# Graph network in four layers: search work kept out of layer 0's drain, row loads issued singly in it, and the scale table computed before the feature gathers

## The chip, the cores and the metric

The kernel runs on one core of a Trainium2 chip. The core has five engines that work side by side, each with its own queue of instructions, which it takes in order: TensorE (PE, matrix products), VectorE (DVE), ScalarE (ACT), GpSimd (POOL) and SyncE (SP, which here only issues transfers). Transfers between memory and the chip run on 16 DMA engines, which all queues share. The metric is the device time of one execution in microseconds, as a median over runs.

## The reference

There are 2708 nodes with 128 features each, and a sparse adjacency matrix with values between 0.05 and 1. Four graph layers follow one another, each of the form x = layernorm(x + layer(x)):

```
layer 0:  hw = x @ W0;  e = leaky_relu((pos @ hw) @ a1)     # pos = adj > 0; nothing is negative
          x = LN(x + (softmax over neighbours of e, times adj) @ hw)
layer 1:  A = adj + I;  D = rowsum(A)
          x = LN(x + relu(D^-1/2 A D^-1/2 (x @ W1.T + b1)))
layer 2:  four-head attention, logits + (1 - adj) * (-1e9)
          x = LN(x + attention(x))
layer 3:  gelu(s_i + d_j + b) for every edge, weighted by adj, summed; an update; two layer norms
```

Layers 0 and 1 are computed with the dense matrix. Layer 2 and layer 3 need each node's neighbours as a list: a row's largest entries and where they stand. Finding these lists is the kernel's "search", and the row sums D for layer 1 come out of it too.

## The kernel before

**Blocks and passes.** Nodes are cut into 22 blocks of 128 rows (`NB`), the output columns into six chunks of 512. A dense layer is done in two passes over the matrix, each accumulating some chunks in PSUM: chunks 0-2 and 3-5 in layer 0, chunks 0-3 and 4-5 in layer 1 (`PASSES`). `half_of(layer, h, ...)` is one pass: for n in 0..21 it multiplies row block n (tile `ah`) with the block's weights; `each(n, ...)` adds what else belongs to a step; `end` does a little work after the first chunk. The second pass holds back the last four row blocks (the first pass, one) and takes them chunk by chunk, so that chunks are complete one after another.

**Row loads.** `load_ahead(limit)` issues loads of row blocks into seven buffers (`BUFFERS`), as far as `limit`. Layer 0's rows and those of layer 1's second pass go through SP's queue. Those of layer 1's first pass are rows in the order of degree, so they are gathered by POOL with an indirect DMA (L728, 1.05 MB each). POOL is in order: a load whose buffer isn't free holds up all that is behind it.

**Finishing.** `finish(layer, blocks, sT)` is a generator that takes four blocks of a complete chunk through the rest of the layer, piece by piece: transposes back on PE (L635), the addition to X on DVE with the row sums (L649, "last sums" in the change), mean on POOL, squares on ACT (L257), the root on POOL (L262), the norm on ACT (L267), transposes on PE (L664), and the projection for the next layer. In layer 0 this projection is written to DRAM as `TH` through ACT's queue (L707); in layer 1 `TA` is written by ACT and `TS`, row by row in order of degree, by POOL (L693). The finishes of a first pass (`later`) run during the steps of the second pass, each starting some steps after the one before. The finishes of the second pass (`drain`) run after it; this stretch is called the drain here. `step()` moves each of them by two pieces.

**Search.** `entries(...)` is one long generator. For each block of rows in order of degree, POOL gathers the full rows (`nat`, L536, 1.39 MB, four buffers), DVE finds the eight largest entries (MAX8, L558; for blocks up to 9 in pieces, L565), the row's sum SD (L577), and the positions of the entries (FIND_INDEX8, L580; two such searches for blocks 1 to 9, three for block 0, one from block 10). After a block's first index search the load of the row block three further on is issued. `search(n)` spends a credit of n; one credit is about one of these 3 us operations. Which search work stands where on DVE's queue is thus fixed by the credits given at each place.

**Layer 1's first pass.** Its weights are the features `HS`, gathered by POOL from TH in order of degree (`features`, L861) and multiplied on ACT by DS = D^-1/2 (`weights`, L866). `given(blocks)` makes DS for some blocks, from SD by a multiply on DVE (L856) and a power on POOL (L857), and calls `search` until their sums are there. In step n the pass gathers features n + 4, gives some search credit, makes DS for blocks n + 2 and n + 3 on even n, and scales features n + 1.

**What fixes the order.** Most instructions go through `pinned(...)`, which ties each to the one before it on its engine, so their order is that in which the program emits them. The stores TH, TA and TS and SP's loads are not pinned; the framework places these as their inputs become ready. Waits come from data and buffers alone.

Of the kernel before, what the change touches and what calls it, by code (L numbers as in the profile page):

```python
# [69 lines left out]
def sparse_path(  # L70
# [29 lines left out]
    NB = -(-N // P)  # L100
# [8 lines left out]
    BUFFERS = 7  # L109
# [490 lines left out]
    with (  # L600
# [23 lines left out]
        def scaled(jb):  # L624

            pinned(S_.activation(H[:, jb, :], H[:, jb, :], AF.Copy, scale=f[:, jb : jb + 1]))  # L626

        def finish(layer, bs, sT):


            n = len(bs)
            g = slice(bs[0], bs[-1] + 1)
            o = pt.tile([P, BANK], F32, name="o_ps")
            for j in range(n):
                pinned(T_.transpose(o[:, blk(j)], sT[:, blk(j)], ident))  # L635
            yield
            if layer:
                y = sb.tile([P, 4, D], F32, name="y1")
                for j, b in enumerate(bs):

                    pinned(V_.scalar_tensor_tensor(
                        y[:, j, :], H2[:, b, :], 1.0, o[:, blk(j)], ALU.mult, ALU.add
                    ))
                for j, b in enumerate(bs):
                    pinned(S_.activation(
                        y[:, j, :], y[:, j, :], AF.Relu, scale=dinv[:, b : b + 1]
                    ))
            for j, b in enumerate(bs):
                pinned(V_.scalar_tensor_tensor(  # L649
                    X[:, b, :], y[:, j, :] if layer else o[:, blk(j)],  # L650
                    1.0 if layer else RZ[:, b : b + 1], X[:, b, :], ALU.mult, ALU.add,
                    accum_out=SUM[:, b : b + 1],
                ))
            squares, norm = norm_sums(bs)
            yield
            yield
            squares()
            yield
            yield
            norm()  # L660
            yield
            o = pt.tile([P, BANK], F32, name="o_ps")
            for j, b in enumerate(bs):
                pinned(T_.transpose(o[:, blk(j)], X[:, b, :], ident))  # L664
            yield
            xt = small.tile([P, BANK], F32, name="xt")
            pinned(S_.copy(xt[:, : n * P], o[:, : n * P]))
            yield
            if layer:

                K = D + 2 * HEADS
                ts = []
                for k in range(0, n, 2):
                    m = min(2, n - k)
                    t = pt.tile([P, BANK], F32, name="q_ps")[:, : 2 * K]
                    ts.append((k, m, t.rearrange("p (b k) -> p b k", k=K)))
                    for i in range(m):
                        pinned(T_.matmul(
                            ts[-1][2][:, i, :], xt[:, blk(k + i)], W2, start=True, stop=True
                        ))  # L680
                yield
                for k, m, t in ts:
                    b = bs[0] + k
                    pinned(S_.copy(XP[:, b : b + m, :], t[:, :m, :]))
                yield
                yield
                nc.scalar.dma_start(
                    TA[bs[0] * P : (bs[-1] + 1) * P, :].rearrange("(b p) c -> p b c", p=P),
                    XP[:, g, : D + HEADS],
                )  # L690

                for b in bs:
                    i = G_.indirect_dma_start(  # L693
                        TS, bass.IndirectOffsetOnAxis(ap=RANK[:, b : b + 1], axis=0),
                        XD[:, b, :], None,
                    )
                    tc.declare_no_dep(i.ins, group="TS", reason="each row has a place of its own")
                    tc.add_to_no_dep_group("TS", i.ins)
            else:

                t = pt.tile([P, BANK], F32, name="q_ps").rearrange("p (b k) -> p b k", k=D)
                for i in range(n):
                    pinned(T_.matmul(t[:, i, :], ONES, B1, start=True, stop=False))
                    pinned(T_.matmul(t[:, i, :], xt[:, blk(i)], W1, start=False, stop=True))
                yield
                pinned(S_.copy(H2[:, g, :], t[:, :n, :]))
                nc.scalar.dma_start(  # L707
                    TH[bs[0] * P : (bs[-1] + 1) * P, :].rearrange("(b p) d -> p b d", p=P),
                    H2[:, g, :],
                )  # L710
            yield
# [3 lines left out]
        loaded, done = [], [0]  # L715
# [24 lines left out]
        def half_of(layer, h, weights, each, end, later):  # L740


            half = PASSES[layer][h]
            lo, hi = span_of(layer, h)
            acc = [
                (pa if i < 3 else pz).tile([P, BANK], F32, name="acc" if i < 3 else "z")
                for i in range(len(half))
            ]
            base = (2 * layer + h) * NB

            def product(n, a, i):
                w = min(BANK, hi - lo - i * BANK)
                pinned(T_.matmul(  # L753
                    acc[i][:, :w], weights[:, n, :], a[:, i * BANK : i * BANK + w],
                    start=n == 0, stop=n == NB - 1,
                ))

            steps = [((1 + 3 * i if layer else 1 + 4 * i), finish(*args)) for i, args in enumerate(later)]
            last = []
            for n in range(NB):  # L760
                now = [s for k, s in steps if k <= n]
                a = loaded[base + n]
                if n < NB - (4 if h else 1):
                    for i in range(len(half)):
                        product(n, a, i)
                else:
                    last.append((n, a))
                each(n, a, lo, hi)
                if not last:
                    done[0] = base + n + 1  # L770
                    load_ahead(base + n + BUFFERS - 1)
                for s in now:
                    next(s, None)
            ends, drain = [], [s for _, s in steps]

            def step():
                for s in list(drain):
                    if next(s, 0) == 0 or next(s, 0) == 0:
                        drain.remove(s)

            for i, c in enumerate(half):
                for m, (n, a) in enumerate(last):
                    product(n, a, i)
                    if not layer:
                        search(0.28)
                    if layer or m % 2:
                        for g in drain:
                            next(g, None)
                w = min(N, (c + 1) * BANK) - c * BANK
                sT = short if w < BANK else sb.tile([P, BANK], F32, name="sT", bufs=4)  # L790
                pinned(S_.copy(sT[:, :w], acc[i][:, :w]))
                ends.append((layer, range(c * 4, min(NB, c * 4 + 4)), sT))
                if i == 0:
                    end()
                if h:
                    drain.append(finish(*ends[-1]))
            done[0] = base + NB
            load_ahead(base + NB + BUFFERS - 1)
            while drain:
                step()  # L800
                if not layer:
                    search(0.55)
            return [] if h else ends

        RZ = lists.tile([P, NB], F32, name="RZ")
        later = []
# [3 lines left out]
        for h, half in enumerate(PASSES[0]):  # L810
# [13 lines left out]
            def each0(n, a, lo, hi, h=h, behind=behind, pattern=pattern):  # L824
                if h == 0 and n + 2 < NB:
                    scaled(n + 2)
                m = signs[n % 2]
                if h and n < 2:
                    nc.gpsimd.memset(m[:, hi - lo :], 0.0)
                pinned(S_.activation(m[:, : hi - lo], a, AF.Sign))  # L830
                if behind:
                    pattern()
                behind.append((n, m))
                if h == 0 and n == 0:
                    order(pt, nat)
                    next(passes)
                if h or n >= 8:
                    search(0.85 if h else 0.8)

            def end0(z=z, blocks=blocks, pattern=pattern):  # L840
# [9 lines left out]
            later = half_of(0, h, H, each0, end0, later)  # L850
# [15 lines left out]
            pinned(S_.activation(HS[:, k, :], HS[:, k, :], AF.Copy, scale=DS[:, k : k + 1]))  # L866

        EARLY = 4
        for k in range(4):
            features(k)  # L870
        given(range(EARLY))
        weights(0)
        for h in range(2):

            def each1(n, a, lo, hi, h=h):
                if h:
                    return
                if n + 4 < NB:
                    features(n + 4)
                search(0.96)  # L880
                k = n + 2
                if EARLY <= k < NB and k % 2 == 0:
                    given(range(k, k + 2))
# [203 lines left out]
    with (  # L1087
# [173 lines left out]
        for k in range(NB):  # L1261
# [8 lines left out]
            if k:  # L1270
                added(k - 1)
                i, j = place[k]
# [526 lines left out]
```

## Time and profile before

| | us |
|---|---|
| median of three runs | 708.85 |
| lowest and highest | 706.58, 709.79 |
| the profiled execution | 709.3 |
| its span, first to last instruction | 707.5 |
| busy in it: PE, DVE, ACT, POOL | 451.2, 393.0, 272.4, 378.5 |

In the profile's time, layer 0's second pass ends with its last products at about 173 us; layer 1's first product starts at 221.75; its first pass ends at about 301; and the gathers of layer 2 begin on POOL at 362.90. A profile lists, for each engine, instructions with their start, length, line in the kernel, output and inputs; the idle time in front of one is put down to the engine or DMA that released it last. The chain of waits follows the execution back from its last instruction, each time to what released the one before.

### The profile page before, as it was taken

What the parts mean: (1) busy time and instruction counts of PE and PEld (TensorE: products, weight loads), DVE (VectorE), ACT (ScalarE), POOL (GpSimd) and SP (SyncE); (2) the same over time, 40 slices, a digit from 0 to 9 for tenths busy, and PEclk for the clock granted to TensorE, in tenths of its full rate; (3) what the DMA queues carried; (4) which work ended last, traced back from release to release, by engine and by line L of the source; (5) the groups of instructions that cost most, each with busy time, mean ns of one, the idle gap of its engine ahead of it and who ended that gap; (6) DMA issues with size and microseconds to landing.
All of it is one profiled execution on the core that took longest, in us unless ns stands there. A gap on an engine that the chain in (4) does not pass through costs nothing.

```text
span 707.5 us, 8193 instructions
## 1 busy us (share of the span) xinstructions
PE 451.2 (64%) x2565; PEld 301.7 (43%) x2565; DVE 393.0 (56%) x1138; ACT 272.4 (38%) x719; POOL 378.5 (53%) x449
## 2 busy tenths in 40 slices
PE   5889999996164999997511502066646546747461
PEld 5745445663152444464311501055536435545451
DVE  4767999999983856640208834111171251434466
ACT  3145655772330100174411574055335424444330
POOL 7002001221246776036577677777777777777761
PEclk9579999998556999999755555566776857788665
DMA  9968999996294999875254111222122122211210
GB/s 296 406 245 309 415 415 379 324 374 224 101 386 153 419 418 415 311 216 191 85 181 128 42 52 40 53 54 52 52 53 55 53 53 53 53 52 52 54 48 13
DMA packets 44400, 128.68 MB, mean 182 GB/s; under 512 B 7983, under 2 KB 19523, under 8 KB 38716
## 3 DMA queue, kind: packets, MB, share of 16 engines
q0 software_dynamic: 16832, 75.13, 30.2%
q1 hardware_dynamic: 21116, 49.66, 19.7%
q10 hardware_dynamic: 6400, 3.29, 1.7%
q8 instruction: 22, 0.36, 0.2%
q14 instruction: 30, 0.25, 0.1%
HBM read 119.29 MB, written 8.81 MB: 181 GB/s over the span
## 4 chain that ended last, share of the span: by engine, by line
DVE 27%; POOL 24%; PE 19%; issue 14%; DMA 9%; ACT 6%; SPq 0%; POOLq 0%; DVEq 0%; ACTq 0%
POOL G L1150 17%; PE acc L753 12%; DVE IX L580 9%; DVE cand L565 5%; DMA G<-TD,LIDX 4%; PE z L753 3%; POOL ga L918 2%; DMA TOP<-in_high 1%; POOL TS L693 1%; ACT squares L257 1%; PE w_ps L355 1%; ACT XD L267 1%; ACT X L1061 1%; DMA nat<-in_adjo,PERM 1%; POOL ln_r L262 1%
## 5 line engine op out<-in xcount | busy, mean ns | idle before, releaser
L1150 POOL DMA_INDIRECT G<-TD,LIDX x187 | 177.4, 948 | 58.7 <-issue 52.4
L1143 PE MATMUL aT_ps<-W,M 128*128 128x128 f32 x418 | 91.0, 394 | 112.5 <-ACT M L1180 105.1
L1143 PEld LDWEIGHTS aT_ps<-W,M 128*128 128x128 f32 x418 | 80.9, 292 | 126.4 <-ACT M L1180 114.0
L1179 DVE TENSOR_TENSOR M<-G,sd_ps 128x1152 f32<-128x1152 f32 (+11 forms) x22 | 28.3, 1287 | 159.0 <-DMA G<-TD,LIDX 142.8
L753 PE MATMUL acc<-ah,XD 128*128 128x512 f32 (+1 forms) x264 | 113.7, 568 | 1.0 <-ACT XD L626 1.0
L580 DVE FIND_INDEX8 IX<-V,nat 128x8 uint32<-128x2707 f32 x33 | 97.8, 2970 | 0.0
L830 ACT ACTIVATE sign<-ah 128x1536 bf16<-128x1536 f32 (+1 forms) x44 | 57.7, 1327 | 37.1 <-issue 26.8
L753 PE MATMUL acc<-ah,HS 128*128 128x512 f32 x132 | 63.3, 615 | 12.1 <-ACT HS L866 12.1
L753 PEld LDWEIGHTS acc<-ah,XD 128*128 128x128 f32 x264 | 47.9, 196 | 44.5 <-issue 41.4
L536 POOL DMA_INDIRECT nat<-in_adjo,PERM x22 | 21.5, 979 | 81.5 <-DVE IX L580 55.4
L1171 ACT ACTIVATE W<-TAB,V 128x128 f32<-128x128 f32 x187 | 56.8, 390 | 0.0
L558 DVE MAX8 V<-nat 128x8 f32<-128x2707 f32 x12 | 35.7, 2976 | 26.6 <-DMA nat<-in_adjo,PERM 26.6
L1180 ACT ACTIVATE M<-sd_ps 128x128 f32<-128x128 f32 x22 | 6.1, 278 | 113.2 <-DVE M L1179 113.2
L753 PEld LDWEIGHTS acc<-ah,HS 128*128 128x128 f32 x132 | 25.4, 196 | 44.7 <-issue 29.3
L866 ACT ACTIVATE HS<-HS,DS 128x128 f32<-128x128 f32 x22 | 8.4, 399 | 78.0 <-DMA HS<-TH,PERM 48.8
L565 DVE MAX8 cand<-nat 128x8 f32<-128x338 f32 (+3 forms) x88 | 34.3, 461 | 2.8 <-DMA nat<-in_adjo,PERM 2.8
L251 POOL TENSOR_SCALAR ln_a<-SUM 128x4 f32<-128x4 f32 (+1 forms) x12 | 2.9, 238 | 61.1 <-DVE XD L649 33.2
L1250 POOL DMA_INDIRECT out_x<-yo,PERM x22 | 22.1, 1003 | 18.5 <-DVE yo L1229 11.3
L861 POOL DMA_INDIRECT HS<-TH,PERM x22 | 21.0, 957 | 19.6 <-DMA TH<-H 10.1
L1052 POOL DMA_INDIRECT TD<-yd,PERM x22 | 24.2, 1102 | 9.6 <-ACT yd L1048 4.1
L753 PE MATMUL acc<-ah,H 128*128 128x512 f32 (+1 forms) x88 | 28.1, 462 | 0.0
L693 POOL DMA_INDIRECT TS<-XD,RANK x22 | 21.6, 982 | 11.3 <-issue 5.4
(281 smaller groups left out, 862.6 us busy)
## 6 DMA issues: line engine op xcount, KB each, us to landing
ah<-in_adjL SPq DMA_DIRECT2D x22, 768.0 KB, 13.5
ah<-in_adjR SPq DMA_DIRECT2D x44, 330.0 KB, 5.5
TOP<-in_high SPq DMA_DIRECT2D x5, 1354.0 KB, 13.0
ah<-in_adjL SPq DMA_DIRECT2D x22, 256.0 KB, 7.2
G<-TD,LIDX POOLq DMA_INDIRECT x187, 2.5
OWN<-TS SPq DMA_DIRECT2D x3, 798.0 KB, 8.5
TA<-XD ACTq DMA_DIRECT2D x5, 264.0 KB, 2.8
TH<-H ACTq DMA_DIRECT2D x5, 256.0 KB, 10.2
```

The costliest lines, as they stand in the source:

```text
L558: pinned(nc.vector.max(V[:, b, 0:8], t))
L565: pinned(nc.vector.max(c[:, 8 * k : 8 * k + 8], t[:, at]))
L580: pinned(nc.vector.max_index(IX[:, b, s], V[:, b, s], t))
L693: i = G_.indirect_dma_start(TS, bass.IndirectOffsetOnAxis(ap=RANK[:, b : b + 1], axis=0), XD[:, b, :], None,)
L753: pinned(T_.matmul(acc[i][:, :w], weights[:, n, :], a[:, i * BANK : i * BANK + w], start=n == 0, stop=n == NB - 1,))
L830: pinned(S_.activation(m[:, : hi - lo], a, AF.Sign))
L1052: i = G_.indirect_dma_start(TD, bass.IndirectOffsetOnAxis(ap=PERM[:, b : b + 1], axis=0), yd[:, i, :], None)
L1143: pinned(T_.matmul(t, a, b, start=n == 0, stop=n == len(parts) - 1))
L1150: pinned(G_.indirect_dma_start(G[:, s, :], None, TD, bass.IndirectOffsetOnAxis(ap=LIDX[:, b, s : s + 1], axis=0),))
L1171: pinned(S_.activation(W[:, s, :], ident, AF.Copy, scale=V[:, b, s : s + 1]))
L1179: pinned(V_.tensor_tensor(M[:, :n, :], G[:, :n, :], s_, ALU.add))
L1250: i = G_.indirect_dma_start(out, bass.IndirectOffsetOnAxis(ap=PERM[:, b : b + 1], axis=0), h, None, bounds_check=N - 1, oob_is_err=False,)
```

## The change

In layer 0's second pass search credit is given only up to step 17, none while the last products are taken chunk by chunk; in the drain it is given from the point where all three finishes have added their sums, one credit per step instead of 0.55. The loads of layer 1's first row blocks are no longer issued together ahead of the drain, but at most one after each of its steps, with the rest after it. The first four blocks' DS is made before the first four feature gathers are issued. In the steps of layer 1's first pass the credit is 1.1 instead of 0.96. The finishes that run during layer 1's second pass start four steps apart instead of three.

```diff
+        added_up = [0]
+
         def finish(layer, bs, sT):
...
                     accum_out=SUM[:, b : b + 1],
                 ))
+            added_up[0] += 1
             squares, norm = norm_sums(bs)
...
-            steps = [((1 + 3 * i if layer else 1 + 4 * i), finish(*args)) for i, args in enumerate(later)]
+            steps = [(1 + 4 * i, finish(*args)) for i, args in enumerate(later)]
...
+            added_up[0] = 0
             for i, c in enumerate(half):
                 for m, (n, a) in enumerate(last):
                     product(n, a, i)
-                    if not layer:
+                    if not layer and not h:
                         search(0.28)
...
             done[0] = base + NB
-            load_ahead(base + NB + BUFFERS - 1)
+            if not h:
+                load_ahead(base + NB + BUFFERS - 1)
             while drain:
                 step()
-                if not layer:
-                    search(0.55)
+                load_ahead(min(base + NB + BUFFERS - 1, len(loaded) + 1))
+                if not layer and added_up[0] >= len(half):
+                    search(1.0)
+            if h:
+                load_ahead(base + NB + BUFFERS - 1)
             return [] if h else ends
...
-                if h or n >= 8:
+                if n < 18 if h else n >= 8:
                     search(0.85 if h else 0.8)
...
         EARLY = 4
+        given(range(EARLY))
         for k in range(4):
             features(k)
-        given(range(EARLY))
         weights(0)
...
-                search(0.96)
+                search(1.1)
```

## The prediction

> **What bounds the kernel now.** I read the page first, then busy time by stages, the chain of waits, and each engine's instructions in order of time from 150 to 366 us. The page gives the time to move, and by the DMA row (40 slices of 17.7 us, in tenths) where transfers are full: slices 3-8 and 13-15, with a hole in 10 and 12 between:
>
> ```profile
> span 707.5 us, 8193 instructions
> DMA  9968999996294999875254111222122122211210
> ```
>
> By stages (columns: stretch, its length, then busy us and instruction count of PE, PEld, DVE, ACT, POOL, then granted clock, DMA share, GB/s):
>
> ```profile
> 175.00:180.00 5.00, 0.00 (x0) 0.00 (x0) 4.76 (x15) 0.00 (x0) 0.00 (x0) 0.53 0.51 214
> 205.00:210.00 5.00, 4.56 (x20) 4.02 (x19) 4.93 (x5) 1.21 (x4) 0.38 (x1) 0.55 1.01 392
> 210.00:215.00 5.00, 0.00 (x0) 0.00 (x0) 2.40 (x3) 0.07 (x1) 0.00 (x0) 0.79 0.68 254
> 215.00:220.00 5.00, 0.00 (x0) 0.00 (x0) 4.45 (x6) 0.00 (x0) 3.62 (x4) 0.50 0.14 39
> 240.00:250.00 10.00, 10.00 (x25) 4.40 (x24) 8.34 (x7) 1.10 (x3) 8.06 (x10) 1.00 1.02 419
> 280.00:285.00 5.00, 5.00 (x13) 2.28 (x12) 2.84 (x1) 0.00 (x0) 2.07 (x3) 1.00 1.00 407
> ```
>
> Two stages, two limits. From 173 to 221 PE has almost nothing: the first product of layer 1 waits for layer 0's drain. From 225 to 295 PE is full and so are the DMA engines, at about 418 GB/s. The drain in the chain of waits (start, us, what):
>
> ```profile
> 179.99 2.76 issue
> 182.75 1.15 DVE XD L649 x8
> ...
> 210.10 4.51 DMA TH<-H
> ...
> 220.21 1.06 POOL DS L857
> ```
>
> And the end of layer 1's first pass, in the instructions in order of time (start, us, instruction, then idle time before it and its releaser):
>
> ```profile
> 282.16 2.98 DVE L558 MAX8 V<-nat 128x8 f32<-128x2707 f32 x1 [2.94 <-DMA nat<-in_adjo,PERM]
> ...
> 289.26 0.71 POOL L857 TENSOR_TENSOR DS<-SD,HALF 128x2 f32<-128x2 f32 x1 [5.90 <-DVE SD L856]
> ...
> 292.74 0.40 ACT L866 ACTIVATE HS<-HS,DS 128x128 f32<-128x128 f32 x1 [3.20 <-DMA HS<-TH,PERM]
> ```
>
> PE had the transposes for blocks 12-15 ready at 169.8, but DVE, 13 us behind with search, added them at 182.75. The last feature store (TH) left at 210.10. Later, block 21's row came at 282.16, its scale at 289.97; PE's step 20 waited for gathered features until 293.1. So that scale has only 2.8 us to spare.
>
> **What the skill says.** DMA: Bandwidth & Descriptors, "Queues, rings and completion order": each DMA engine takes turns between queues, packet by packet, so small stores share with big loads. The trace agrees: the TH store issued at 203.25 landed after 10.2 us, beside row loads that ended at 213.1; the last, at 210.10, landed with them gone at 214.61. Same page, "Where 436 GB/s comes from": a ceiling of 435; the trace's 419 is near it, so bytes moved into 225-295 cost time. TensorE: Matmul & The Clock Gate, "Part 1: The HAM clock gate": an idle window of some 3.4 us halves the clock and as much work restores it. Trace: 0.50 at 215-225, 1.00 from 230.
>
> **The change, part by part.**
>
> *Search out of the drain.* Between block 8's candidates and the last sums, before ran on DVE: two index searches each of blocks 8 and 9 and one of block 10 (5 x 2.97), candidates of 9 (4.2), MAX8 of 10 (2.97), about 22 us. After, DVE is free at 165.5. Walking the queues with the trace's durations: add 12-15 at 170.0-171.1, sums on POOL to 171.7, ACT squares (behind a copy of sums that ends at 172.1) to 173.6, POOL roots 1.6 to 175.3, norms 1.65 to 177.0, squares 16-19 to 178.5, roots to 180.2, norms to 181.9; PE transposes and products as before (1.6 + 3.4 a group at half clock, 1.7 for the last pair). Last TH issue about 191 instead of 210.1: 19 us.
>
> *Row loads one by one.* Before, five loads stood on POOL at 192.5-198.6 ahead of the roots of 16-19. After, load 1 follows the last sums at 181.1, then nat 11, and the last pair's root; loads 2-4, nat 12 (after block 9's first index search, 189.1) and load 5 end at about 191.5. But 5 x 1.05 + 2 x 1.386 = 8.0 MB then fill the DMA from 182.6: 19.2 us at 418 GB/s, to about 202.5. All three TH stores fall into that. They crawl as at 203.25 and land at about 204.3, not 196. Gain at the first feature gather 215.47 - 205.2 = 10.3 us, not 19. Lower bound of that landing: 197 (191 plus the 6.5 us of the store at 207.76); upper: 207.
>
> *Scale table first.* Its POOL power (1.06) now waits for DVE through block 10's MAX8, 195; the gathers are queued behind it, but wait for TH until 204 anyway, so it costs nothing. It takes 1.3 us of POOL from behind the gathers, so gather 4 moves from 221.45 to about 210.3: 11.1 us gained. Were TH to land at once, this wait would set a floor of 196.
>
> *What moved into layer 1.* At its start before had MAX8 of block 12 behind it, after only that of block 10: four DVE operations (12 us) and nat loads 13 and 14 move in. Credit 1.1 instead of 0.96: 1.1 x 3.1 = 3.4 us of DVE a step, against PE's 3.43: DVE isn't the limit in between. But nat 21 is issued in step 15, not 13. Ahead of it in POOL's queue are 2 more nat, 2 more row and 2 more feature loads: 2 x (1.386 + 1.049 + 0.066) = 5.0 MB = 12.0 us. SP's loads for the next pass start when step 15's product frees a buffer, and now overlap it: about 3 of 0.34 MB, 2 us. Nat 21 lands at 282.16 - 11.1 + 12.0 + 2.0 = 285.1. From there as before 7.8 us (MAX8, index, scale, power): 292.9, step 20 at 293.4 against 293.29. The lead is eaten. And since PE finished step 19 some 8 us earlier, its clock falls: step 20 takes 5.3 instead of 3.43, +1.9. End of the pass: +2.0 us.
>
> *Layer 1's finishing every 4 steps.* PE's queue is in order. Before, the transposes of 12-15 stood before step 17 and ran at 333.0 behind POOL's stores TS (5.1 us a group); the four last products of chunk 4 ended at 339.8. After, that finish starts at step 13, not 10: its root, norm, transposes and projection stand just before those four products. Laying out POOL, ACT and PE by the same durations (step 1.105, norms 1.65, relu 1.28, root 1.64, stores 1.26 each) gives, for before, sums of 16-19 at 344.2 (trace 344.6). For after, on the same origin: norms of 12-15 at 335.1, chunk 4's copy at 343.0 instead of 339.6, sums of 16-19 at 346.2: +2.0. PE idles less in mid-pass, but step 17 was not the end. The stores aren't pinned; I place them as the trace does, as soon as their projection is copied. If they interrupt less, the cost is -0.5; if they stand behind the sums, +6.4. I take +2.0.
>
> The remaining edits are free: in layer 1's second pass no rows are left to load, so the load calls between its drain's steps issue nothing, and SP's queue keeps its order everywhere.
>
> The terms no trace shows, with both ends: TH's landing 197 to 207 (nat 21 7 us earlier to 3 later; but a pass more than some 6 us shorter is barred by the features, which then bind), SP's overlap 0 to 3, the clock 0 to 1.9, finishing -0.5 to +6.4. All at one end: 709.3 - 6 - 0.5 = 703, and 709.3 + 2.0 + 2.7 + 1.0 + 6.4 = 721.
>
> Sum: 709.3 for the profiled execution (span 707.5 and 1.8 around it) + 2.0 + 2.0 = 713.3; the median 708.85 is 0.45 below that execution, so 712.9.
>
> **Rivals.** (1) *The lead survives; not slower.* If TH stores slip between the loads and land near 198, everything to nat 21 comes 6 us earlier, step 20 is then bound by its feature gather, PE idles less and keeps its clock: pass -4 to -6, finishing 0 to +2. Time 705, down to 701. For it: at 208 us most of a group's store went through within 1 us, with a load pending. Against: from 157 to 161 stores and loads in one queue after another moved side by side, 10.2 and 15.0 us to land. It decides where TH lands before 201. (2) *The layer 1 spacing costs more*: stores behind the sums, +6.4 instead of 2: 717, and 719 with TH at 207. For it: four operations of a finish queue behind POOL's 5.1 us blocks. Against: before's stores went out early. (3) *It cancels*: stores and clock cost nothing, 709. (4) *DVE is no hindrance*: the drain was bound elsewhere, no gain: then before's 13 us lag would not show; 3 in 100, about 717.
>
> **Numbers.** Forecast 712.9 has 0.42 (its own range 710 to 716), rival 1 0.25, rival 2 0.17, rival 3 0.13, rival 4 0.03. A measurement tells about 0.5%, 3.5 us, from no change: faster 0.25; same, rival 3 and two fifths of the forecast, 0.30; slower 0.45. Range 701 to 719 leaves out some 0.15.
>
> **What would show it.** Right: adds of 12-15 near 170; last TH issue near 191 but landing beyond 202; first gather near 205; nat 21 landing near 285 and DVE the last wait of step 20, clock below 1 after it; TS stores ahead of sums. Wrong: TH landing below 199, step 20 waiting for its features, or chunk 4's copy no later after the pass's start.

## The result, and the profile after

The changed kernel takes 717.06 us, the median of four runs (714.57 to 717.35); the kernel before, beside it, 707.72 (706.3 to 709.79). The ratio is 1.0117, 95% interval 1.0097 to 1.0137: slower by 9 us. The forecast was 712.9 with a range of 701 to 719, some 4 us more than before. Its direction and its chain of causes were right; two terms of its sum were too small. The profiled execution took 717.35 with a span of 715.6, 8.1 more than the span before.

The events the forecast named, in us from the start of the span:

| event | before | forecast | after |
|---|---|---|---|
| PE's transposes of blocks 12-15 done | 169.8 | as before | 171.5 |
| DVE adds blocks 12-15 | 182.75 | 170.0 | 171.5 |
| last TH store issued | 210.1 | 191 | 190.1 |
| TH landed | 214.6 | 204.3 | 207.4 |
| first feature gather issued | 215.5 | 205.2 | 208.3 |
| search row of block 21 landed | 282.2 | 285.1 | 288.8 |
| step 20 of layer 1's first pass | 293.2 | 293.4 | 297.1 |
| second pass begins | 300.9 | 302.9 | 307.0 |
| chunk 4 copied, after that beginning | 39.1 | 42.1 | 44.6 |
| sums of blocks 16-19, after that beginning | 43.7 | 45.3 | 48.0 |

In the first row this execution is 1.7 us late. PE waits for nothing there; eight products from 162.36 took 6.64 us, before 5.15, because the granted clock in 165-170 was 0.67 instead of 0.99. It is scatter and not the change: in the twelve executions of the changed kernel and of its variants below, none of which is edited ahead of that place, DVE's first add came anywhere from 169.94 to 172.79. So differences of absolute times under some 2 to 3 us between two traces say little; those from one event to another in the same trace are firmer.

The page of the kernel after, span and transfers (40 slices of 17.9 us):

```profile
span 715.6 us, 8195 instructions
DMA  9968999990669999476227111222122222211210
```

Counted from 0, slice 9 (161 to 179 us) now moves almost nothing; 10 and 11 stand at six tenths, where before 10 stood at two, 11 at nine and 12 at four; transfers are full from 12 to 15 instead of 13 to 15. The stages show the same (columns as before: length, then PE, PEld, DVE, ACT, POOL, then clock, DMA share, GB/s):

```profile
180.00:185.00 5.00, 4.17 (x19) 4.17 (x20) 5.00 (x7) 3.67 (x12) 3.36 (x7) 0.50 0.00 0
...
200.00:205.00 5.00, 0.00 (x0) 0.00 (x0) 4.93 (x5) 0.00 (x0) 0.00 (x0) 0.50 1.02 421
205.00:210.00 5.00, 0.00 (x0) 0.00 (x0) 4.93 (x7) 0.00 (x0) 1.40 (x2) 0.50 0.34 135
210.00:215.00 5.00, 3.64 (x5) 1.58 (x6) 2.16 (x2) 1.49 (x4) 3.78 (x5) 0.50 0.20 52
...
280.00:285.00 5.00, 2.66 (x6) 1.25 (x7) 4.63 (x5) 0.40 (x1) 1.08 (x2) 1.00 1.04 423
```

PE's drain is over by 190, 20 us sooner. Then PE has nothing for 21 us, for 17 of which the transfers run at some 421 GB/s. And in 280-285, where before PE was full, it now works 2.66 us of 5, with the DMA engines still full. The chain of waits names both places:

```profile
190.06 17.37 DMA TH<-H
...
272.99 15.81 DMA nat<-in_adjo,PERM
288.82 2.99 DVE V L558
...
295.93 0.73 POOL DS L865
...
297.13 4.97 PE acc L756 x6
```

The last TH store takes 17.37 us beside the row loads; before, issued after them, it took 4.51. At the end of the pass stands block 21's row, 15.81 us on its way, and behind it DVE and POOL. The instructions behind that row in order of time (start, us, instruction, idle time and its releaser):

```profile
292.18 2.97 DVE L580 FIND_INDEX8 IX<-V,nat 128x8 uint32<-128x2707 f32 x1
295.68 0.16 DVE L864 TENSOR_SCALAR SD<-SD 128x2 f32<-128x2 f32 x1
295.93 0.72 POOL L865 TENSOR_TENSOR DS<-SD,HALF 128x2 f32<-128x2 f32 x1 [13.30 <-DVE SD L864]
297.13 2.07 PE L756 MATMUL acc<-ah,HS 128*128 128x512 f32 x2 [7.62 <-ACT HS L874]
```

PE stands for 7.62 us. Its six products of that step then take 4.97 us instead of 2.84: the clock has fallen, to 0.50 in 295-300. Earlier in the pass PE had already waited three times for gathered features that were late, 1.49 us at 263, 1.52 at 272 and 3.02 at 282; in the kernel before it waited for nothing between its first product and the second pass. The index search at 292.18 stands ahead of the scale although the scale doesn't use it.

The second pass, before and after, in the same view, cut to the instructions that matter here; TS are POOL's stores, `ln_a` the means of a finish, and the x10 the products that stand behind the finish of 12-15 and end chunk 4:

```profile
323.62 0.23 POOL L251 TENSOR_SCALAR ln_a<-SUM 128x4 f32<-128x4 f32 x1
336.39 3.85 PE L753 MATMUL acc<-ah,H 128*128 128x512 f32 x10
340.02 0.58 ACT L791 COPY sT<-acc 128x512 f32<-128x512 f32 x1 [3.05 <-DMA TA<-XD]
344.63 0.27 POOL L251 TENSOR_SCALAR ln_a<-SUM 128x4 f32<-128x4 f32 x1
```

and after:

```profile
327.53 0.96 POOL L696 DMA_INDIRECT TS<-XD,RANK  x1 [0.30 <-issue]
328.51 0.28 POOL L251 TENSOR_SCALAR ln_a<-SUM 128x4 f32<-128x4 f32 x1
336.92 0.96 POOL L696 DMA_INDIRECT TS<-XD,RANK  x1 [0.30 <-issue]
337.90 0.27 POOL L251 TENSOR_SCALAR ln_a<-SUM 128x4 f32<-128x4 f32 x1
342.44 1.63 PE L667 MATMUL o_ps<-TAB,XD 128*128 128x128 f32 x4 [4.74 <-ACT XD L267]
346.72 5.11 PE L756 MATMUL acc<-ah,H 128*128 128x512 f32 x10
351.61 0.58 ACT L795 COPY sT<-acc 128x512 f32<-128x512 f32 x1 [4.26 <-PE acc L756]
354.97 0.23 POOL L251 TENSOR_SCALAR ln_a<-SUM 128x4 f32<-128x4 f32 x1 [2.67 <-DVE XD L651]
```

The means of blocks 12-15 ran 22.7 us after the pass began (323.62); now they run 30.9 us after it (337.90), directly behind four stores, and PE waits 4.74 us for their norm with the last products of chunk 4 still to come. After that wait PE is slow as well: the projection took 2.18 us instead of 1.09 and those ten products 5.11 instead of 3.85, with a clock of 0.58 in 345-350. The last `ln_a` line of each list is the mean of 16-19, the last row of the table.

By the parts: the first pass ends 6.1 us later, the second is 4.3 longer, and 2.2 come back after layer 1: from the first table gather to the end of the span it is 344.6 us before and 342.4 after. The eight executions below on chips of this speed, with edits only ahead of that place, took 340.8 to 343.8, so the profiled execution of before was itself a slow one there.

### The profile page after: what moved, and what is told of

Read it like the earlier page. It is cut to its first block, busy times and chain, and to the rows that moved or that the text cites. A ratio compares the mean times of both kernels' runs of the same rounds, so it can differ in the third digit from the quotient of the medians.

```text
span 715.6 us, 8195 instructions
## 1 busy us (share of the span) xinstructions
PE 453.4 (63%) x2565; PEld 300.8 (42%) x2565; DVE 393.1 (55%) x1138; ACT 272.8 (38%) x719; POOL 379.1 (53%) x449
## 4 chain that ended last, share of the span: by engine, by line
POOL 25%; PE 24%; DMA 20%; issue 13%; DVE 11%; ACT 6%; SPq 1%; POOLq 0%; DVEq 0%; ACTq 0%
POOL G L1158 17%; PE acc L756 17%; DMA ah<-in_adjL,PERM 6%; DMA G<-TD,LIDX 4%; DMA TOP<-in_high 3%; DMA TH<-H 2%; POOL ga L926 2%; DMA nat<-in_adjo,PERM 2%; PE z L827 2%; ACT squares L257 2%; POOL ln_r L262 1%; ACT X L1069 1%; ACT XD L267 1%; DVE M L1187 1%; PE aT_ps L1151 1%
## 5 line engine op out<-in xcount | busy, mean ns | idle before, releaser
L756 PE MATMUL acc<-ah,HS 128*128 128x512 f32 x132 | 65.5, 634 | 35.4 <-ACT HS L874 35.4
L731 POOL DMA_INDIRECT ah<-in_adjL,PERM x22 | 21.5, 979 | 13.7 <-issue 5.0
L926 POOL DMA_INDIRECT ga<-TA,LIDX x22 | 23.9, 1085 | 6.7 <-issue 6.7
```

Source lines behind the costliest of these rows:

```text
L756: pinned(T_.matmul(acc[i][:, :w], weights[:, n, :], a[:, i * BANK : i * BANK + w], start=n == 0, stop=n == NB - 1,))
L926: pinned(G_.indirect_dma_start(ga[:, i, :], None, TA, bass.IndirectOffsetOnAxis(ap=LIDX[:, b, 0:1], axis=0)))
```

## Experiments

The theory: (a) from 215 to 290 the transfers are the limit, so an earlier start of layer 1 is worth nothing unless bytes are moved out of that stretch too, and the changed order moves bytes in; (b) DVE's index search then stands in the way of the last scale; (c) the 4-step spacing costs time of its own in the second pass. The main rivals: the start of layer 1 decides, and the spacing is free. Ratios are to the kernel before, run beside each variant; the changed kernel's own ratio is 1.0117.

### The spacing of layer 1's finishing

```
-            steps = [(1 + 4 * i, finish(*args)) for i, args in enumerate(later)]
+            steps = [((1 + 3 * i if layer else 1 + 4 * i), finish(*args)) for i, args in enumerate(later)]
```

> The changed kernel with layer 1's finishing every 3 steps again, all else as changed. My theory: the 4-step spacing alone makes the second pass of layer 1 longer; in the traces the sums of blocks 16-19 came 43.7 us after that pass began before the change and 48.0 after it. With 3 steps they come back to 43-44.5 us and the time falls by 3.5 to 4.5 us against the changed kernel, to about 713. Rival: the spacing is free, and the second pass is longer only because it began late and at a low clock: the sums stay at 47-48 us, the time within 1 us of 717.

Measured: 1.0041 (1.0017 to 1.0064) against 1.0117. The second pass began at 306.2, nearly as late as in the changed kernel and with step 20 as slow (4.91), and the sums came 43.7 us after it, exactly as before. The rival falls.

The same line the other way round in the kernel before:

> The kernel before with the 4-step spacing in layer 1 as its only change. My theory: sums of blocks 16-19 at 46-48 us after the second pass begins instead of 43.7, all else up to there as before, and 2.0 (as the prediction laid out) to 4.3 us (as the trace after shows) more: 710 to 712. Rival: the spacing costs nothing by itself: 707-708.5.

Measured: 1.0030 (1.0007 to 1.0053), sums at 47.4 us instead of 43.7. PE had its full clock at the end of the first pass here, so the late and slow end of that pass isn't part of it: in the traces the spacing costs 3.8 to 4.3 us by itself, about double what was laid out. In the times it is less sharp, 0.5 to 3.8 us here by the interval, some 5 us where it was undone. Why it costs that much was asked of the TS stores, each of which was put in a step of its own:

```
                 for b in bs:
-                    i = G_.indirect_dma_start(
+                    i = pinned(G_.indirect_dma_start(
...
-                    )
+                    ))
...
-                    tc.add_to_no_dep_group("TS", i.ins)
+                    tc.add_to_no_dep_group("TS", i.ins); yield
```

> The changed kernel with the TS stores of layer 1's finish put one to a step, in an order fixed on POOL, so that one of blocks 0-3 instead of four stands ahead of the means of 8-11, and six instead of eight ahead of the means of 12-15. Theory: it is these stores of 1.26 us that make the 4-step spacing cost 4 us: the norm of 12-15 and the last products move 1.3 to 2.5 us forward and the sums of blocks 16-19 come 45.5 to 46.7 us after the second pass begins instead of 48.0: 714.5 to 716. Rival: POOL's stores aren't in the way: 48 us and 717.

The instructions of POOL in that run:

```profile
324.82 1.10 POOL L696 DMA_INDIRECT TS<-XD,RANK  x1 [0.56 <-ACT XD L267]
327.54 0.23 POOL L251 TENSOR_SCALAR ln_a<-SUM 128x4 f32<-128x4 f32 x1 [1.62 <-DVE XD L651]
336.56 0.27 POOL L251 TENSOR_SCALAR ln_a<-SUM 128x4 f32<-128x4 f32 x1
353.26 0.23 POOL L251 TENSOR_SCALAR ln_a<-SUM 128x4 f32<-128x4 f32 x1 [1.35 <-issue]
```

The means of 8-11 no longer wait for stores. In the changed kernel DVE had their sums at 326.2 and the means ran at 328.51, 2.3 us later. The pass began at 308.24, so the sums of 16-19 came 45.0 us after it, 3.0 less than in the changed kernel: by the trace the stores are most of the spacing's price. The remaining 1.3 us were not taken apart; PE still waited 4.42 us for the norm of 12-15 and was slow after it. The time neither shows nor denies it: the ratio of 1.0116 has an interval of 1.0074 to 1.0157, wider than the effect. This run and the last three that follow (rows together, all rows together, one search row) ran on two other chips, where the kernel before took 787 and 795 us. In their traces the extra time lies in layer 3, and up to 370 us they run as elsewhere; for these four only the ratio and the trace are read.

### The last scale behind an index search

```
                     summed[0] = b + 1
+                    if b == NB - 1: yield 0.0
...
             while summed[0] <= bs[-1]:
-                search(0.5)
+                due[0] += 0.5
+                while due[0] > 0.0 and summed[0] <= bs[-1]: due[0] -= next(passes)
```

> The changed kernel, but the scale of the last two blocks (20, 21) stands ahead of block 21's index search on DVE, which it doesn't need. My theory: step 20 of layer 1's first pass waits for DVE through that one search of 2.97 us; the scale comes at about 292.7 instead of 295.7, step 20 starts at about 294.2 instead of 297.1, the pass ends 3 to 3.5 us sooner and the time is about 714. Rival: the transfers or PE's clock set that end, not DVE: step 20 starts within 1 us of 297 and the time stays at 716-718.

Measured: 1.0047 (1.0030 to 1.0063), 5 us less than the changed kernel. The end of the pass, in order of time:

```profile
289.32 2.98 DVE L558 MAX8 V<-nat 128x8 f32<-128x2707 f32 x1 [4.06 <-DMA nat<-in_adjo,PERM]
...
292.98 0.72 POOL L865 TENSOR_TENSOR DS<-SD,HALF 128x2 f32<-128x2 f32 x1 [9.92 <-DVE SD L864]
...
294.19 2.84 PE L756 MATMUL acc<-ah,HS 128*128 128x512 f32 x6 [2.60 <-ACT HS L874]
```

The row came as late as ever, but PE idled 2.60 us instead of 7.62 and kept its clock there: the step took 2.84 us, not 4.97. The second pass began at 301.9 instead of 307.0. So 3 us of the end are DVE's order and 2 its echo in the clock, and the rival falls. With the spacing at 3 as well:

> The changed kernel with both mended: layer 1's finishing every 3 steps, and the last scale ahead of block 21's index search. If the two costs are separate, they add: the second pass begins at 301-302.5 (before: 300.9) and the sums of blocks 16-19 come 43.7 us after that: 707.5 to 710, a ratio of 1.000 to 1.004 to the kernel before. That would show that the change's gain of 8 us at the start of layer 1 comes to nothing at the end of the first pass, even with both costs gone. Rival: the gain was only covered by them: 703 or less.

Measured: 1.0005 (0.9992 to 1.0019), second pass at 302.6, sums at 43.8. In the trace the two costs are separate, each as large as alone. The ratios of the two single runs would add up to 0.997; the 0.003 that are missing are about what the four intervals allow together. With both costs gone, layer 1's earlier start (first gather 207.9 against 215.5) still gives nothing at the end: the rival of 703 falls.

### What an earlier start is worth, and what the transfers are worth

The loads between the drain's steps were left out and came in step 0 of layer 1, behind the gathers:

```
                 step()
-                load_ahead(min(base + NB + BUFFERS - 1, len(loaded) + 1))
...
-            if h:
+            if h and layer:
                 load_ahead(base + NB + BUFFERS - 1)
```

> The changed kernel without row loads in layer 0's drain: the five are issued in step 0 of layer 1, behind the first five feature gathers. Only two search rows (2.8 MB) then move beside the TH stores. Theory on the stores (small packets take turns with the big ones of the loads): the last TH store lands at 193-197 instead of 207.4 and the first feature gather is issued at 197-199 instead of 208.3. Theory on the worth of it (from 215 to 290 the transfers are the limit, and the five row loads, 12.5 us of transfer, now begin at 204 instead of 183, which eats the 11 us gained): block 21's row lands within 3 us of 288.8 and the time within 3 us of 717. Rival (the start of layer 1 decides): first gather 10 us earlier, block 21's row near 279, time 707-710. Rival on the stores (they are slow in themselves): TH still lands at 205-208.

Measured: 1.0112 (1.0075 to 1.0150). POOL and DVE in order of time:

```profile
195.99 1.04 POOL L865 TENSOR_TENSOR DS<-SD,HALF 128x4 f32<-128x4 f32 x1 [8.92 <-DVE SD L864]
197.22 1.03 POOL L869 DMA_INDIRECT HS<-TH,PERM  x1 [0.19 <-issue]
...
290.29 2.98 DVE L558 MAX8 V<-nat 128x8 f32<-128x2707 f32 x1 [4.02 <-DMA nat<-in_adjo,PERM]
```

The gathers go out 11 us sooner and don't even wait for TH; now the scale table ahead of them is what they stand behind. So the stores are slow only beside the row loads. PE's first product, too, comes 11 us sooner, at 200.40. But its second step waits for a row load:

```profile
212.89 5.28 PE L756 MATMUL acc<-ah,HS 128*128 128x512 f32 x6 [6.92 <-DMA ah<-in_adjL,PERM]
```

In the changed kernel that step began at 217.24, so of the lead 4.4 us are left; block 21's row lands at 290.3, later than with the late gathers, and the time is what it was. The edit moves two things at once, the start forward and five row loads (5.2 MB, 12.5 us at 419 GB/s) back, and from 195 to 205 hardly anything moved (13 and 52 GB/s). It doesn't price an earlier start alone, which no run does. It shows that a start that is bought with later transfers is worth nothing here, as theory (a) says, against the rival of 707 to 710.

The opposite: leave the start, and fill the transfers' hole. The search rows of blocks 13 to 15 are issued ahead of the gathers, where POOL stands waiting for TH anyway:

```
         given(range(EARLY))
+        while summed[0] < 13: search(0.5)
         for k in range(4):
```

> The changed kernel with search rows 13 to 15 issued on POOL ahead of the feature gathers, which stand there waiting for TH. In the trace after, POOL had nothing to do from 197.4 to 208.3 and the transfers had run out at about 203, while row 13 was only issued at 214.6, behind five gathers. Theory (the transfers set when block 21's row lands): rows 13, 14, 15 go out at about 197.5, 199.6 and 206; the TH store, which shares with them, lands 2 to 4 us later (209-212 instead of 207.4); block 21's row lands at 281-284 instead of 288.8, step 20 no longer waits for DVE for long and PE keeps its clock; the second pass begins at 298-301 instead of 307.0 and the time is 708-711. Rival: TH is held up by as much as is gained (landing at 214 or later): the second pass begins after 304 and the time is 714-718.

```profile
204.49 0.94 POOL L536 DMA_INDIRECT nat<-in_adjo,PERM  x1 [5.28 <-DVE IX L580]
215.47 0.95 POOL L869 DMA_INDIRECT HS<-TH,PERM  x1 [10.04 <-DMA TH<-H]
...
270.46 2.98 DVE L558 MAX8 V<-nat 128x8 f32<-128x2707 f32 x1 [1.74 <-DMA nat<-in_adjo,PERM]
```

The first line is block 15's row. TH is held up to 214.6, as the rival said (its last store takes 26.12 us in the chain of waits), and the first gather goes out at 215.47, as late as in the kernel before. DVE gains no work by it: in the changed kernel it had done with block 12 by 212 and stood 9.18 us for the row of block 13. So only the order of transfers differs. Yet block 21's row lands at 270.5, 18 us sooner and further than the theory's 281 to 284 (one may think that the pass's row loads wait for buffers of a PE that began 7 us later, and left the transfers to the search rows; that wasn't tried). PE doesn't wait for it, the second pass begins at 298.6, 8.5 us before the changed kernel's (1.6 of these may be scatter, as DVE's adds came at 169.96 instead of 171.53), and the ratio is 1.0029 (1.0014 to 1.0044). So with all of the gain at the start given away, the first pass ends sooner than in either kernel. With the spacing at 3 and the scale first as well:

> The changed kernel with all three: search rows 13 to 15 ahead of the feature gathers, finishing every 3 steps, the last scale ahead of block 21's index search. Theory: block 21's row at 281-284, step 20 bound by PE alone, the second pass beginning at 296-298.5 (before: 300.9) and its sums 43.7 us later: 703 to 706, faster than both kernels. Rival: transfers or features bind at the same place as before: 707-710.

Measured: 0.9973 (0.9951 to 0.9995), second pass at 299.6 (theory: 296 to 298.5), sums 43.9 after it. The median, 706.7, lies just past the theory's band: PE is the bound, as it said (it waits 1.51 and 0.17 us in the pass), but began late because TH landed at 214.8, where the expectation for the run above had 209 to 212.

Then the loads one by one were undone, so that the hole before 183 is filled:

```
-            if not h:
+            if 1:
                 load_ahead(base + NB + BUFFERS - 1)
             while drain:
                 step()
-                load_ahead(min(base + NB + BUFFERS - 1, len(loaded) + 1))
```

> The changed kernel with the five row loads of layer 0's drain issued together, as the kernel before did, instead of one by one behind the drain's steps. On POOL they then stand at about 178.3-184.3, ahead of the roots of blocks 16-19 (180.4 in the trace after), where one by one they stood at 183.2-193.6; from 172 to 183 nothing moved at all. Theory (the transfers set when block 21's row lands): roots 4 us later, the last TH store issued at about 194 instead of 190.1, but the row loads begin 5 us earlier and are gone by 198 instead of 203; TH lands at 200-204 instead of 207.4, block 21's row at 282-285, and the second pass begins at 298-302 instead of 307: 709 to 712. Rival (the later roots and stores decide): TH lands at 207 or later and the time is 717-720.

Measured: 1.0054 (1.0032 to 1.0076), half of the changed kernel's loss gone. The chain of waits has

```profile
195.66 8.71 DMA TH<-H
```

and the stages

```profile
180.00:185.00 5.00, 3.35 (x14) 3.06 (x14) 5.00 (x7) 0.52 (x2) 3.97 (x6) 0.50 0.95 352
...
200.00:205.00 5.00, 0.00 (x0) 0.00 (x0) 4.93 (x5) 0.00 (x0) 0.00 (x0) 0.50 0.43 138
```

The last store goes out 5.6 us later than in the changed kernel and lands 3.0 sooner, at 204.4, because the loads are gone sooner: 352 GB/s in 180-185 where there was nothing. Block 21's row lands at 285.6 and the second pass begins at 303.6, 3.4 sooner. The gain at the pass's end is less than the theory's 5 to 9.

One run was to show what SP's loads for the next pass cost that row:

```
...
-                    load_ahead(base + n + BUFFERS - 1)
+                    load_ahead(base + (NB if layer and not h and n < 18 else n + BUFFERS - 1))
...
                     given(range(k, k + 2))
+                    if k + 2 == NB: pinned(nc.sync.dma_start(dram.tile([1, 2], F32, name="HOLD"), DS[0:1, k : k + 2]))
```

> The changed kernel with SP's row loads for layer 1's second pass held back until the last scale (blocks 20 and 21) is there; a 8-byte store of that scale stands ahead of them on SP. In the trace after, four of them (0.338 MB each, 1.35 MB, 3.2 us at 418 GB/s) moved beside block 21's row, which took 15.8 us. Theory: that row lands 3 us sooner, at about 286, step 20 begins near 294 with PE's clock not yet halved, and the time is 711-713, as when the scale alone was moved. The first row of the second pass lands at about 299, before it is wanted at 302. Rival: the row isn't slowed by them: 288-289 and 716-718. Where the held loads come too late, the second pass waits for them at its start: 717 or more.

Measured: 1.0163 (1.0144 to 1.0182). It is inconclusive on the time, because the first line shown also let this pass's own row loads run two rows further ahead: these 2 x 1.049 MB stood in POOL's queue ahead of the search rows, and block 21's was issued at 277.40 instead of 272.99. From its issue it then took 13.34 us instead of 15.81, so SP's loads, which began only at 299 here, had cost it about 2.5 us; that is an estimate, because the two row loads stood ahead of it here and behind it there. The 4.4 us of the later issue are theory (a) once more: two rows in front of it are 5.0 us at 418 GB/s.

### All together

> Search rows 13 to 15 ahead of the feature gathers, finishing every 3 steps, the last scale ahead of block 21's index search, and the five row loads together. Theory: the 12 us without transfers before 183 are used as well; TH lands at 205-209 instead of 214-215, the second pass begins at 292-295 instead of 299.6: 697 to 701, ratio 0.986 to 0.992. Rival: TH is held up to 213 again: 704-707.

Measured: 0.9897 (0.9855 to 0.9940), faster than the kernel before, and so than the changed one. The chain of waits where TH lands:

```profile
195.10 14.88 DMA TH<-H
```

TH landed at 210.0, a little past the theory's 205 to 209; the second pass began at 293.9, 7.0 us before the kernel before and 13.1 before the changed one, and the sums came 43.7 after it. PE waited once, 1.28 us, between its first product and that pass.

Last, with `summed[0] < 11` in place of 13, so that less moves beside the stores:

> As the run before with all four edits, but only search row 13 ahead of the feature gathers instead of rows 13 to 15: 2.77 MB less beside the TH stores. Theory (the small stores finish with the loads beside them): TH lands at 203-206 instead of 210, the first gather is issued at 204-207 instead of 210.9; block 21's row comes 6 to 8 us later than its 265.9, still early enough, and PE, which bounds the pass, begins the second pass at 288-291.5 instead of 293.9: 2.5 to 6 us less, a ratio to the kernel before of 0.980 to 0.987. Rival: the transfers that are put off make PE wait for its rows in mid-pass: the second pass begins at 293-296, a ratio of 0.989 to 0.994.

Measured: 0.9953 (0.9933 to 0.9972). The theory's first half held, its second fell. The gather went out at 206.5, but the rows put off came back later (PE, in order of time):

```profile
265.41 2.84 PE L756 MATMUL acc<-ah,HS 128*128 128x512 f32 x6 [1.54 <-ACT HS L874]
274.21 2.84 PE L756 MATMUL acc<-ah,HS 128*128 128x512 f32 x6 [1.67 <-ACT HS L874]
285.12 4.54 PE L756 MATMUL acc<-ah,HS 128*128 128x512 f32 x6 [3.44 <-ACT HS L874]
```

Block 21's row landed at 281.2 instead of 265.9, twice as much later as reckoned, PE waited again and again (these are the three longest) and was slow after the last of them, 4.54 us instead of 2.84, and the second pass began at 298.0, past even the rival's 293 to 296. Again 4.4 us at the start were worth less than bytes moved early. The ratio, too, lies past the rival's.

## Why the prediction was right, and where its sizes were off

- **DVE's lag, and the 19 us.** Right: adds at 171.5, just behind PE's transposes; the last TH issue 20.0 us sooner.
- **TH lands beside the loads.** Right in kind, 3.1 us short. The 19.2 us of loads were counted from 182.6. The first one was issued at 183.2, but nothing moved in 180-185 and only 335 GB/s in 185-190 (1.68 MB), so counted at 421 GB/s they began at about 186.0, 3.4 us late; half of that is this execution's own lateness. The stores' own 0.66 MB, 1.6 us, had been left out: 8.0 + 0.66 MB at 421 GB/s from 186.0 end at 206.6. That is the first mis-sized term.
- **Scale table first, free.** Right: its power ran at 196.4, with 11 us to spare; where TH came early (rows behind the gathers) it set the floor that the prediction gave, 196.
- **Block 21's row eats the lead.** Right: it landed 3.7 us later than forecast, 3.1 of them from the late gathers. The experiments made this the centre: it is the transfers that bind the pass. SP's overlap, taken at 2 us, came to about 2.5 by the estimate above.
- **From the row to the scale 7.8 us, clock 1.9.** Right: 288.82 to 296.65 is 7.83, and the slow step cost 2.1. PE's wait ahead of it was 7.6 us.
- **End of the first pass +2.0.** It was +6.1. The 4.1 between are the row's 3.7 (late start of transfers, the stores' bytes, the execution's own 1.7) and small rests of the chain. (For step 20 before, the prediction has 293.29, from the chain of waits; the instruction starts at 293.19.)
- **Finishing every 4 steps, +2.0.** Right that it costs, half the size: 3.8 to 4.3. The layout by durations put chunk 4's copy at 42.1 us; it came at 44.6. Groups of four stores ran straight ahead of the means of 8-11 and of 12-15 and held each by 2.3 us, and after the wait for the norm of 12-15 PE worked slowly, which a layout by the durations at full clock leaves out: the projection and the ten products behind it took 7.3 us instead of 4.9. That is the second mis-sized term.
- **The sum.** The two passes lost 10.4 us where 4.0 were forecast. 709.3 + 6.1 + 4.3 = 719.7 against the 717.35 of the profiled execution; the 2.2 us in layers 2 and 3 are what the reference execution had been slow by. The prediction didn't know of them. With the passes as they came its own sum, 719.7, lies past the upper end of its range, so that the time lies inside is in part luck.
- **Rivals.** The time is the 717 of the second rival, but only 2.3 of the 4.4 us that it added came from the spacing. The first (the lead survives where TH lands before 201) can't be tried in its own terms, as TH didn't land early beside the loads; in the one run with TH landed by 197 the row loads came later, and the time was no better. Among the variants of the changed kernel the second pass began earlier than with the last scale moved alone (301.9) only in the four runs in which search rows were moved forward (293.9 to 299.6).

The prediction took the row loads one by one as they came and asked only whether they hold up TH. The runs showed that their order costs in itself: together they start 5 us sooner, and the pass ends 3.4 us sooner.

## What to carry to other kernels

Where the DMA engines are full through a stage, don't count on an earlier start of that stage alone; look for the stretch ahead of it in which they stand still, and for a load there that is ready but queued behind a waiting instruction. Count the transfers from the first byte moved, not from the issue, and count the small stores in. Before delaying a load to spare a small store, reckon what the same bytes cost later: here gathers 11 us sooner, with the row loads behind them, gained nothing, and three search rows issued early gained 8.5 us at the end of the pass with gathers 7 us later.

## What the runs showed of the hardware

- The last store to TH, 128 KB, took 4.5 us where the loads beside it ended 3 us after its issue, and 8.7, 14.9, 17.4 and 26.1 us where they went on for longer. It landed from 2 us after to 2 us before the end of the transfers beside it. In the changed kernel one sees why: from 190 to 204 the queue of the stores and that of the loads moved packet for packet, 695 packets beside 685, but 0.35 MB beside 5.56. In the run with the search rows first it was 604 beside 605 from 192 to 204. It isn't always so: in the kernel before, from 208 to 210, 418 packets of stores passed beside 73 of loads. What decides between these was not tried.
- PE's clock doesn't go by the length of a wait alone. In the changed kernel's trace a wait of 3.02 us at 282 left the step at 2.84 us; in the run with spacing 3 and the scale first, 3.01 us at the same step made it 4.54, and 2.50 us later on 4.31, where the run with the scale first alone had 2.60 and 2.84. So the prediction's window of some 3.4 us is no safe limit: waits well below it cost the clock in some executions. What decides between them was not tried.
- After the first row load's issue at 183.22 nothing moved until 185.0, and some 410 GB/s were reached only in 187-188. Counted at full rate that is a start 2.8 us after the issue, longer than the 2.5 us that the 1.049 MB of one row then take at 418 GB/s.
